# Counting kept context rows: adding six comparison tables on VectorE before TensorE sums them over the partitions

## The chip, the cores and the metric

The kernel runs on one NeuronCore of a Trainium2 chip. The metric is the device time of one execution in microseconds. The engines are TensorE (PE, its weight loads PEld), VectorE (DVE), ScalarE (ACT), GpSimd (POOL) and SyncE (SP); each has a queue of its own that it works through in order, and semaphores tie the queues together.

## The reference

A gated cross-attention block followed by a gated feed-forward network whose two layers have rounded activations and ternary weights. There are 16 batch elements with 224 tokens of width 512 and up to 750 context rows of width 384; a mask says for each batch element which context rows count. Cut to what matters:

```python
x = x + tanh(g_xattn[0]) * cross_attention(layernorm(x), ctx, mask, W_q, W_k, W_v, W_o, b_o)   # 8 heads of 64
x = x + tanh(g_ffn[0]) * ffn(layernorm(x), w1, b1, w2, b2)

# cross_attention
sim = einsum('bihd,bjhd->bhij', q, k) * scale
sim = where(mask[:, None, None, :], sim, max_neg)
out = einsum('bhij,bjhd->bihd', softmax(sim), v)

# ffn: twice a linear layer of this kind, with an exact gelu between them
xq = act_quant(rmsnorm(x))     # rounded to 255 levels per row
wq = weight_quant(w)           # rounded to -1, 0, 1 times the mean of |w|
einsum('bsd,fd->bsf', xq, wq) + b
```

Masked rows get a weight of zero, so only the kept rows of the context need be fetched and computed with.

## The kernel before, in words

**Ordering the batch.** `order_batches` (lines 30 to 159) counts the kept rows of each batch element, sorts the 16 elements by that count into slots, and gives each slot a capacity: 192 kept rows for the first eight slots, 128 for the last eight (`CAPS`, line 26). It also makes `sh.upto`: with the 750 rows laid out as 6 columns on 125 partitions, it holds for each row and slot how many rows are kept up to and including that row. If every slot fits its capacity, `compact_path` (from line 726) does the rest.

**select(s)** (line 809) turns these counts into the places of the kept rows. The place of the k-th kept row is the number of rows whose count is at most k. So for each of the six columns (`NJ`) a VectorE `tensor_scalar` compares the 192 or 128 possible places with the counts, one per partition (line 816, table `ind`, bf16, 125 partitions), and TensorE sums the tables over partitions and columns: the table is the stationary operand, a column of ones the moving one, and six matmuls with one moving column accumulate into one column of PSUM `pi` (line 822). A slot of 192 places takes two such columns (128 and 64 places), so 12 matmuls; one of 128 takes 6. Then `keys` (line 833) clips and shifts the sums to row numbers in memory, and `mask` (line 845) is the additive mask of the slot.

**gather(s)** (line 850) fetches the kept rows by indirect DMAs issued from GpSimd with `keys` as row numbers. The x rows (`fetch`, issued at line 793) and the results (line 1310) go through the same queue. `context_pieces` transposes the gathered rows (line 881) and computes the keys (892) and values (907, 918); `query_pieces` transposes x (987) and computes the queries (1008).

**Attention.** `scores` (line 1037) makes the score matmuls (1047), the masked minimum on VectorE (1061), the exponentials on ScalarE (1071), the reciprocal of the sum `rec` (1080) and the scaling of p on GpSimd (1081). `turn_probs` transposes p on TensorE (1101, 1108), `weighted` applies it to the values (1126, 1141).

**Feed-forward.** Finished tokens are taken in pairs of 128: `project` (1189, 1192), `normalise` (1226 to 1247), `up` (matmuls hp at 1259 into a wide PSUM tile, read by VectorE as `h` at 1267), `gelu` (1279 to 1298), `down` (1304, 1308).

**Weights.** w1 and w2 are loaded in eight pieces each; the first load waits until the first gathered context has landed (line 1347). Their absolute values are summed (1363, 1367, 1373), the scale `sw` comes from the sum (1375 to 1379), and each piece is rounded on VectorE (1396 to 1398) and turned on TensorE (1409, 1413).

**The order of the work.** select(0) and select(1) stand at the head of the compact path (lines 1464 and 1466), select(2) after the first sum of weights (line 1495), and stage s of the main loop (line 1505) holds select(s + 3), merged with the attention pieces of s, the queries and keys of s + 1, and the feed-forward or weight pieces. From this program order a planner makes the order of each engine's queue: an instruction whose operands and buffer it expects to be ready may pass earlier ones, and a buffer is handed on when its last reader is done. `ind` has one buffer, so the tables of a slot can only be built when the matmuls of the slot before have read theirs.

**The counters.** `evict` (line 757) sends each copy out of PSUM to VectorE or ScalarE, whichever has the smaller sum of charged work in `load`. Other code adds its own charges to `load["v"]` and `load["s"]` in program order; select adds 6 * 170 to `load["v"]`.

Of the kernel before, what the change touches and what calls it, by code (L numbers as in the profile page):

```python
# [9 lines left out]
BF16 = mybir.dt.bfloat16  # L10
AF = mybir.ActivationFunctionType
ALU = mybir.AluOpType
# [713 lines left out]
def compact_path(ctx, tc, sh, x, context, out, late_loads):  # L726

    nc = tc.nc
    P = 128
# [5 lines left out]
    NJ = 6  # L735
    TJ = J // NJ
# [12 lines left out]
    pa = ctx.enter_context(tc.tile_pool(name="pa", bufs=1))  # L749
# [3 lines left out]
    load = {"v": 0.0, "s": 0.0}  # L753
# [14 lines left out]
    def gen(shape, dtype, name):  # L768
        return ps_gen.tile(shape, dtype, tag="gen", name=name)
# [36 lines left out]
    def rows_of(s, t):  # L806
        return min(CAPS[s] - t * P, P)

    def select(s):

        st = live[s]
        cap = CAPS[s]
        nt = 2 if cap > P else 1
        ind = pa.tile([TJ, NJ, 192], BF16, tag="ind", name=f"ind_{s}", bufs=1)
        for n in range(NJ):
            nc.vector.tensor_scalar(ind[:, n, :cap], sh.place[:TJ, :cap], sh.upto[:, n, s : s + 1], None, ALU.is_ge)
        load["v"] += 6 * 170
        pi = gen([P, 2], F32, f"pi_{s}")
        for t in range(nt):
            rows = rows_of(s, t)  # L820
            for n in range(NJ):
                nc.tensor.matmul(
                    pi[:rows, t : t + 1],
                    lhsT=ind[:, n, t * P : t * P + rows],
                    rhs=sh.one[:, 0:1],
                    start=(n == 0),
                    stop=(n == NJ - 1),
                )

        keys = pa.tile([P, 2], I32, tag="keys", name=f"keys_{s}", bufs=3)  # L830
        for t in range(nt):
            rows = rows_of(s, t)
            nc.vector.tensor_scalar(
                keys[:rows, t : t + 1],
                pi[:rows, t : t + 1],
                float(J - 1),
                sh.first[:rows, s : s + 1],
                ALU.min,
                ALU.add,
            )  # L840
        st["keys"] = keys

        mb = pa.tile([TQ, 320], F32, tag="mask", name=f"mask_{s}", bufs=1)
        nm = 320 if nt > 1 else P
        nc.vector.tensor_scalar(
            mb[:, :nm], sh.place_f[:TQ, :nm], sh.slots[:TQ, 0, s : s + 1], -FMAX, ALU.is_ge, ALU.mult
        )
        st["mask"] = mb
# [613 lines left out]

    fetch(0)
    select(0)
    gather(0)
    select(1)
    norm_first(0)
    with tc.issue_after(norm_first(1)):
# [14 lines left out]
    with ExitStack() as behind:  # L1483
        for instruction in latest.values():
            behind.enter_context(tc.issue_after(instruction))
        scores(0, 0)
        scores(0, 1)
        for _, piece in queries[3:] + keys_values[3:]:
            piece()
        for c in range(NPC):  # L1490
            sum_weights(0, c)
        scale_weights(0)
        for _, piece in norm_pieces(1):
            piece()
        select(2)

        held = [sh.wo[0:1, 0, 0:1], sh.wo[0:1, 2, 0:1], sh.wo[P // 2 : P // 2 + 1, 2, 0:1]]
        for dst in held + [sh.bo[0:1, 0:1], sh.b1[0:1, 0:1], sh.b2[0:1, 0:1]]:
            nc.scalar.copy(dst, weight_sums[0][0:1, NPC - 1 : NPC])
# [85 lines left out]
```

## Time and profile before

| what | us |
|---|---|
| median of the three runs | 757.25 (756.26 to 759.62) |
| profiled execution, its own time | 755.32 |
| profiled execution, span from first to last instruction | 753.5 |
| busy: TensorE, VectorE, ScalarE, GpSimd | 680.1, 505.9, 407.6, 397.0 |
| granted TensorE clock, mean | 0.976 |

Line numbers with an L are those of the kernel before. A group's mean duration contains the time in which an instruction overlaps its neighbours, so the length of a block of like instructions is read from the timeline. A row of a timeline gives the start, the length, engine, line, operation, tiles and count, and in brackets the idle time of the engine ahead of it and what ended it.

### The profile page before, as it was taken

Reading aid. Unit: us, or ns where it says so; the run is one execution under the profiler, and the core shown is the slowest. Engines: PE = TensorE matmul, PEld = TensorE weight load, DVE = VectorE, ACT = ScalarE, POOL = GpSimd, SP = SyncE. Lnnn points to the kernel's source line nnn. Section 1 sums busy time; section 2 is a strip of 40 time slices with the busy share of each in tenths; the row PEclk is TensorE's granted clock in tenths of the full one; section 3 lists DMA queues with packets and bytes.
Section 4 is the critical chain, followed back from the end, with each engine's and each line's share of the span. In section 5 each row is a group of like instructions: output and inputs, shape, how many; then the busy total and the mean of one; then the engine's idle time right before and its main releaser. Section 6 shows DMA issues by size and latency. Waiting matters only on the chain.

```text
span 753.5 us, 11378 instructions
## 1 busy us (share of the span) xinstructions
PE 680.1 (90%) x3902; PEld 432.9 (57%) x3902; DVE 505.9 (67%) x1300; ACT 407.6 (54%) x960; POOL 397.0 (53%) x543
## 2 busy tenths in 40 slices
PE   4997799999999999997999999999999999988652
PEld 3875587666566566555655575666666666443221
DVE  5598765877484784665768676588594939586860
ACT  1556564384663855736657369266565656460530
POOL 6583567464564644647266564565654453536141
PEclk9998999999999999999999999999999999999887
DMA  6874031132223322222142323123122222213150
GB/s 193 314 267 156 11 90 45 15 73 56 69 47 70 82 56 57 67 57 81 28 99 67 71 67 68 32 77 80 58 57 70 56 70 57 71 28 77 35 113 31
DMA packets 87218, 58.77 MB, mean 78 GB/s; under 512 B 75488, under 2 KB 75632, under 8 KB 87024
## 3 DMA queue, kind: packets, MB, share of 16 engines
q1 hardware_dynamic: 79024, 32.00, 18.8%
q0 software_dynamic: 8128, 25.96, 11.1%
q8 instruction: 33, 0.54, 0.3%
q14 instruction: 33, 0.27, 0.1%
HBM read 32.26 MB, written 7.34 MB: 53 GB/s over the span
## 4 chain that ended last, share of the span: by engine, by line
PE 57%; DVE 12%; issue 10%; POOL 9%; DMA 5%; ACT 2%; POOLq 0%; ACTq 0%; DVEq 0%; SPq 0%
PE qp L1008 9%; PE op L1189 9%; PE fp L1304 8%; PE hp L1259 6%; PE kp L892 5%; PE sim L1047 4%; PE vp L907 4%; PE ptp L1101 3%; PE av L1126 3%; DVE a L1282 2%; POOL p L1081 2%; DVE h L1267 2%; DMA raw<-in_L_ffn_w_dram 2%; DMA hqT<-hq 2%; DVE hq L1285 1%
## 5 line engine op out<-in xcount | busy, mean ns | idle before, releaser
L1081 POOL TENSOR_TENSOR p<-p,rec 112x768 f32<-112x768 f32 (+1 forms) x64 | 84.2, 1318 | 74.8 <-DVE rec L1080 29.6
L1304 PE MATMUL fp<-w2T,hqT 128*128 128x512 fp8e4 x448 | 104.2, 387 | 13.8 <-DMA hqT<-hq 13.7
L1259 PE MATMUL hp<-w1T,xqT 128*128 128x512 fp8e4 x448 | 107.0, 383 | 8.8 <-DVE h L1267 6.2
L1071 ACT ACTIVATE p<-p,nm 112x192 f32<-112x192 f32 (+1 forms) x256 | 106.4, 419 | 11.5 <-DVE nm L1061 11.3
L1008 PE MATMUL qp<-xnT,wq_sb 128*128 128x224 f32 x512 | 104.9, 358 | 0.6 <-ACT xnT L766 0.6
L1189 PE MATMUL op<-wo_sb,xoT 128*128 128x512 f32 x224 | 103.7, 599 | 0.0
L1008 PEld LDWEIGHTS qp<-xnT,wq_sb 128*128 128x128 f32 x512 | 96.8, 193 | 6.4 <-issue 3.3
L1267 DVE SCALAR_TENSOR_TENSOR h<-hp,c,b_bc 128x1024 f32<-128x1024 f32 x56 | 71.6, 1280 | 39.9 <-PE hp L1259 37.4
L1061 DVE CUSTOM_DVE_ANT_0 p<-sim,mask 112x192 f32<-112x192 f32 (+1 forms) x256 | 67.7, 319 | 33.9 <-PE sim L1047 33.4
L1304 PEld LDWEIGHTS <-hqT 128*128 128x128 bf16 x448 | 43.3, 99 | 71.0 <-DMA hqT<-hq 16.9
L1282 DVE TENSOR_REDUCE a<-h 128x1 f32<-128x2048 f32 x28 | 63.9, 2282 | 22.4 <-ACT h L1279 22.3
L1259 PEld LDWEIGHTS <-xqT 128*128 128x128 bf16 x448 | 43.2, 98 | 57.7 <-issue 15.4
L1308 DVE SCALAR_TENSOR_TENSOR y<-fp,c,y 128x512 f32<-128x512 f32 x28 | 20.9, 746 | 76.3 <-PE fp L1304 73.0
L1310 POOL DMA_INDIRECT out_dram<-y,token x28 | 30.9, 1104 | 75.6 <-DVE y L1308 70.6
L1290 ACT ACTIVATE h<-h 128x2048 f32<-128x2048 f32 x28 | 53.4, 1907 | 22.1 <-DVE hq L1285 14.7
L1279 ACT ACTIVATE h<-h 128x2048 f32<-128x2048 f32 x28 | 53.5, 1909 | 19.6 <-DVE k L1200 10.6
L1189 PEld LDWEIGHTS op<-wo_sb,xoT 128*128 128x128 f32 x224 | 40.6, 190 | 38.9 <-issue 36.4
L892 PE MATMUL kp<-ctxT,wk_sb 128*128 128x192 f32 (+1 forms) x384 | 60.9, 306 | 0.0
L892 PEld LDWEIGHTS kp<-ctxT,wk_sb 128*128 128x128 f32 x384 | 55.2, 192 | 6.2 <-issue 4.3
L1247 POOL TENSOR_TENSOR y<-y,b_bc 128x512 f32<-128x512 f32 x28 | 36.6, 1311 | 37.9 <-DVE fx L1228 37.6
L766 ACT COPY pT<-ptp 128x448 f32<-128x448 f32 x63 | 32.7, 536 | 42.6 <-PE ptp L1101 41.3
L1101 PE MATMUL ptp<-ident,p 112*128 112x112 f32 x256 | 36.1, 268 | 17.6 <-POOL p L1081 17.5
(165 smaller groups left out, 1191.4 us busy)
## 6 DMA issues: line engine op xcount, KB each, us to landing
raw<-in_L_ffn_w_dram SPq DMA_DIRECT2D x16, 512.0 KB, 5.6
wq_sb<-in_L_xattn_W_q_dram SPq DMA_DIRECT2D x1, 1024.0 KB, 5.8
b_bc<-in_L_ffn_b_dram SPq DMA_DIRECT2D x1, 1024.0 KB, 7.8
wk_sb<-in_L_xattn_W_k_dram SPq DMA_DIRECT2D x1, 768.0 KB, 7.4
wv_sb<-in_L_xattn_W_v_dram SPq DMA_DIRECT2D x1, 768.0 KB, 8.8
wo_sb<-in_L_xattn_W_o_dram SPq DMA_DIRECT2D x1, 512.0 KB, 3.8
wo_sb<-in_L_xattn_W_o_dram SPq DMA_DIRECT2D x2, 256.0 KB, 5.6
x<-in_x_dram,token POOLq DMA_INDIRECT x28, 3.6
```

The lines of the kernel that those rows point to most:

```text
L892: nc.tensor.matmul(pk[:, p - p0, :], lhsT=sh.wk[:, c, p * P : (p + 1) * P], rhs=st["ctxT"][:, c, :cap], start=(c == 0), stop=(c == NC - 1),)
L1008: nc.tensor.matmul(pq[:, i, :], lhsT=sh.wq[:, d, (p + i) * P : (p + i + 1) * P], rhs=st["xnT"][:, d, :], start=(d == 0), stop=(d == ND - 1),)
L1061: nc.vector.tensor_tensor_reduce(out=probs[:, h, :cap], in0=sim[:, j, i, :cap], in1=st["mask"][:, j * begin : j * begin + cap], scale=-(DH ...
L1071: nc.scalar.activation(probs[:, h, :cap], probs[:, h, :cap], AF.Exp, bias=nmax, scale=-1.0, accum_out=total[:TQ, h : h + 1],)
L1081: nc.gpsimd.tensor_tensor(probs[:, :, :cap], probs[:, :, :cap], rec[:TQ].unsqueeze(2).to_broadcast([TQ, 4, cap]), ALU.mult,)
L1101: nc.tensor.transpose(pt[:, h, :], probs[:, h, c : c + P], ident[:TQ, :TQ])
L1189: nc.tensor.matmul(po, lhsT=xoT[:, d, at : at + P], rhs=sh.wo[:, d, :], start=(d == 0), stop=(d == ND - 1))
L1259: nc.tensor.matmul(ph[:, n, :], lhsT=f["xqT"][:, k * ND + d, :], rhs=w1T[:, d, at : at + NB], start=(d == 0), stop=(d == ND - 1),)
L1267: nc.vector.scalar_tensor_tensor(h[:, cols], ph.rearrange("t i n -> t (i n)"), f["c1", k], sh.b1[:, cols], ALU.mult, ALU.add)
L1279: nc.scalar.activation(f["h", k], f["h", k], AF.Gelu)
L1282: nc.vector.tensor_reduce(amax[:, k : k + 1], h, AX.X, ALU.max, apply_absolute_value=True)
L1304: nc.tensor.matmul(po, lhsT=f["hqT", k][:, n, :], rhs=w2T[:, n, :], start=(n == 0), stop=(n == NF - 1))
```

## The change

Instead of six tables side by side, one table is built. A `tensor_scalar` compares the places with the first column's counts; five `scalar_tensor_tensor` then each compare the places with the next column's counts and add the table so far, in place. The sums are small whole numbers (0 to 6), exact in bf16. TensorE then sums one table over the partitions, so a slot of 192 places takes two matmuls and one of 128 takes one. The table has two buffers in place of one (each a sixth of the former size), and select charges 6 * 260 to VectorE's counter in place of 6 * 170.

```diff
-        ind = pa.tile([TJ, NJ, 192], BF16, tag="ind", name=f"ind_{s}", bufs=1)
-        for n in range(NJ):
-            nc.vector.tensor_scalar(ind[:, n, :cap], sh.place[:TJ, :cap], sh.upto[:, n, s : s + 1], None, ALU.is_ge)
-        load["v"] += 6 * 170
+
+        ind = pa.tile([TJ, 192], BF16, tag="ind", name=f"ind_{s}", bufs=2)
+        nc.vector.tensor_scalar(ind[:, :cap], sh.place[:TJ, :cap], sh.upto[:, 0, s : s + 1], None, ALU.is_ge)
+        for n in range(1, NJ):
+            nc.vector.scalar_tensor_tensor(
+                ind[:, :cap], sh.place[:TJ, :cap], sh.upto[:, n, s : s + 1], ind[:, :cap], ALU.is_ge, ALU.add
+            )
+        load["v"] += 6 * 260
         pi = gen([P, 2], F32, f"pi_{s}")
         for t in range(nt):
             rows = rows_of(s, t)
-            for n in range(NJ):
-                nc.tensor.matmul(
-                    pi[:rows, t : t + 1],
-                    lhsT=ind[:, n, t * P : t * P + rows],
-                    rhs=sh.one[:, 0:1],
-                    start=(n == 0),
-                    stop=(n == NJ - 1),
-                )
+            nc.tensor.matmul(
+                pi[:rows, t : t + 1], lhsT=ind[:, t * P : t * P + rows], rhs=sh.one[:, 0:1], start=True, stop=True
+            )
```

## The prediction

> **What bounds the kernel now.** I read the page first (busy shares and the chain that ended last):
>
> ```profile
> PE 680.1 (90%) x3902; PEld 432.9 (57%) x3902; DVE 505.9 (67%) x1300; ACT 407.6 (54%) x960; POOL 397.0 (53%) x543
> ...
> PE 57%; DVE 12%; issue 10%; POOL 9%; DMA 5%; ACT 2%; POOLq 0%; ACTq 0%; DVEq 0%; SPq 0%
> ```
>
> TensorE is busy for 90% and carries 57% of the chain; VectorE carries 12%. An average says little, so next the busy time by stage (core, then length, then PE, weight load, VectorE, ScalarE, GpSimd):
>
> ```profile
> 37.20:46.40 9.20, 7.35 (x64) 5.01 (x64) 8.69 (x35) 2.52 (x10) 6.88 (x10) 1.00 0.83 268
> 46.40:157.00 110.60, 100.56 (x726) 76.30 (x727) 82.57 (x237) 64.27 (x176) 67.17 (x60) 0.95 0.28 82
> 157.00:540.00 383.00, 368.98 (x2103) 232.45 (x2102) 255.33 (x664) 227.84 (x536) 209.42 (x284) 1.00 0.28 65
> ```
>
> From 46 to 540 us TensorE is the bound (91% and 96%). From 37.2 to 46.4 us VectorE is (94%): the w1 weights have landed, and TensorE waits for the first rounded piece. After 540 us no select is left. Third, the tables and sums themselves, by tile:
>
> ```profile
> L822 PEld LDWEIGHTS <-ind x144: 95/98/157, 9.0 to 533.7; 125*128 125x128 bf16 x96, 125*64 125x64 bf16 x48
> L822 PE MATMUL pi<-one,ind x144: 163/170/210, 9.1 to 533.8; 125*128 125x1 bf16 x96, 125*64 125x1 bf16 x48
> L816 DVE TENSOR_SCALAR ind<-place,upto x96: 226/254/1780, 8.7 to 497.5; 125x192 bf16<-125x192 bf16 x48, 125x128 bf16<-125x128 bf16 x48
> ```
>
> 144 matmuls of 170 ns would be 24.5 us, which misleads: they overlap. TensorE's timeline gives what they occupy:
>
> ```profile
> 80.84 0.58 PE L822 MATMUL pi<-one,ind 125*128 125x1 bf16 x12
> 81.35 0.79 PE L881 MATMUL ctxp<-ident,ctx 128*128 128x128 f32 x3
> ```
>
> Twelve hold TensorE from 80.84 until the next matmul starts at 81.35, 0.51 us; in a later select six hold it from 244.31 to 244.47, 0.16 us. Last, VectorE's timeline in its own stage:
>
> ```profile
> 38.85 0.97 DVE L816 TENSOR_SCALAR ind<-place,upto 125x192 bf16<-125x192 bf16 x5
> 39.85 0.42 DVE L763 COPY v_rest<-vr 128x256 f32<-128x256 f32 x1
> 40.19 0.15 DVE L1377 TENSOR_SCALAR wmean<-wtotp 128x1 f32<-128x1 f32 x1
> ...
> 42.23 1.04 DVE L816 TENSOR_SCALAR ind<-place,upto 125x192 bf16<-125x192 bf16 x5
> 43.19 0.73 DVE L1396 TENSOR_SCALAR raw<-raw,sw 128x1024 f32<-128x1024 f32 x1
> 44.35 0.33 DVE L833 TENSOR_SCALAR keys<-pi,first 128x1 int32<-128x1 f32 x2 [0.43 <-PE pi L822]
> 44.61 0.68 DVE L1397 TENSOR_SCALAR w<-raw 128x1024 int16<-128x1024 f32 x1
> ```
>
> Two blocks of tables stand ahead of the weights here, and nothing hides them.
>
> [...]six of 192 columns take 1.17 us and six of 128 take 1.06, so 64 columns cost 18 ns each time. [...]The trace shows such blocks (3.65 and 4.00 us for six tables, at 433 and 494 us, while GpSimd ran tensor_tensors). [...]here (0.30-0.17)/5 = 26 ns in the blocks of six, (0.58-0.17)/11 = 37 ns in those of twelve.
>
> **The change, part by part.** Against the profiled execution: span 753.5 us, its own time 755.32; the median 757.25 is 1.9 above that, and I carry the difference over.
>
> *TensorE.* A select of the first eight goes from 12 matmuls to 2, of the last eight from 6 to 1. Saved: 0.51 less 2 x 0.04 = 0.43 us, and 0.16 less 0.04 = 0.12. Selects 0 to 3 lie where TensorE waits anyway (before 46 us): nothing, because the waits for the gathered context and the rounded weights cover it. Selects 4 to 6 (80.8, 116.8, 148.7 us): 3 x 0.43 x 0.91 = -1.2 us. Select 7 and the eight short ones: (0.43 + 8 x 0.12) x 0.96 = -1.3 us.
>
> *VectorE, price of the new instruction.* The trace has no such form between SBUF operands of this size. Scalar_tensor_tensor on 32 columns of SBUF takes 193 ns (L151), 512 columns 746 and 1024 columns 1280 (L1308, L1267, one input in PSUM): the slope is 1.043 ns a column. From the 193: 360 ns at 192 columns, 293 at 128. Bounds: down the slope from the 746, 412 and 345[...]. Each link waits for the one before: in the chain a dependent VectorE instruction follows 0.02 us after the one it needs (k at 223.63, its input done at 223.61). So a block is 0.27 + 5 x 0.38 = 2.17 us for 1.17, and 0.26 + 5 x 0.315 = 1.83 for 1.06: +1.00 eight times, +0.77 eight times, 14.2 us more VectorE work.
>
> *Where it lies.* Select 0: keys later by 1.00, less the 0.34 of matmuls no longer run after the last table (10.49 against 9.85, some 0.3 for the two that stay): 0.66 us. GpSimd, which issues the gather, is busy with the x fetches until 12.6 and starts it at 12.88, while keys are ready at 10.86: hidden in 2 us. Select 1 delays the first norm's statistics from 13.05 by 0.6; its next step stands behind the second tile's, which waits for its DMA until 15.03: hidden. Without these covers they cost 0.7 and 0.6. Two x fetches stretched to 1.26 and 1.52 us beside the tables, against 1.02 alone, may also shorten, by up to 0.7. I take 0 for the opening.
> Select 2: the block 38.60 to 39.82 grows by 0.96, and with it v_rest, wmean and sw. Select 3 by 0.87. L1396 comes 1.8 later, but the 0.43 that keys waits for pi is then covered: +1.4 us at L1397, the cast after it and TensorE's first turn of weights (46.34, which already waits 1.7).
> Selects 4 to 15: 4 x 1.00 + 8 x 0.77 = 10.2 us. Behind them in VectorE's queue stand rec (L1080), which frees GpSimd's product for the transposes of p, and h (L1267), which frees the wide PSUM tile for the hp matmuls. At 197 us the third hp starts 4 us after the h that it needs, and GpSimd's product stands behind a DMA wait, so most is hidden. I take VectorE's share of the chain, 12%: +1.2 us.
>
> *Planner and buffers.* Select charges 6 x 260 for 6 x 170. Walking the two counters in program order gives 21 evictions on VectorE before, as in the profile, and 15 after: 12 leave (about 5.3 us at their rows) and five come (3.0 us), all but one before 150 us. Net 2 us from VectorE to ScalarE (54% busy): 0. Two small tables instead of one large one add no DMA and no tile wait; they permit building a table a select earlier. The instruction order of each queue may be remade with that.
>
> Sum: 0 + 1.4 + 1.2 - 1.2 - 1.3 = +0.1 us, so 757.3.
>
> **The rivals.** *Faster (30%).* The second buffer takes select 3's block out of the 37 to 46 us stage (1.3 and the 0.43 wait), less select 2's 0.96: -0.8. The opening gains its 0.7, the chains of VectorE hide fully, TensorE gains all 2.7: -4.2 us, 753.0. If sw and L1396 are moved ahead of the blocks too, 3 us more, 750. For it: VectorE is busy for 10.2 of the 20.8 us from 16.4 to 37.2. Against: the order of today leaves ready work late as well (x fetched at 23 to 26 us has its statistics at 40.26).
> *Slower (24%).* [...]Place: between keys and h. Price: 2.6 to 2.9 us for a block of six at 433 and 494 us. Half of that, 1.4 us, reaching hp decides (3.8 us) from three such collisions beyond today's; four give +5.6, 763. Against: only two of sixteen blocks are hit so hard now, and part was hidden.
> *It doesn't do what it says.* If the matmuls taken out only let TensorE wait elsewhere, nothing stands against +1.4 and +1.2: 759.9, still within the forecast's range and counted there.
>
> **How the numbers follow.** Half a per cent, 3.8 us, is about what this measurement can tell from no change (the three runs span 3.4). Forecast 46%, with its own range 754.5 to 760.5 from the price bounds (5 x 0.05 us a block either way, and 0 to 25% of 10 us reaching the path). The cases of both signs push the range to 751 to 763, leaving a tenth on each side.
>
> **What would show it.** L822 with 24 matmuls; L816 with 16 and the new line with 80 of about 360 and 293 ns; VectorE's busy time up some 12 us (14.2 less 2.3), TensorE's down some 6 (2.7, and about 1 in each of the four selects that it runs while waiting); the first turn of weights near 47.7 us. Wrong if: [...]that turn comes earlier than 46.3; the new line's longest times exceed 1 us in more than three blocks; or the remade order moves a stage between 46 and 540 us by more than 3 us.

## The result and the profile after

The change makes the kernel slower: 778.28 us (776.21 to 781.14, six runs) against 756.75 (754.51 to 759.62, six runs), a ratio of 1.0284 with a 95% interval of 1.0259 to 1.0308. The profiled execution took 777.65 us, its span 775.9. Line numbers behind the change are one lower than before (L1081 is now L1080). The page of the kernel after, busy shares, granted clock and chain:

```profile
PE 687.3 (89%) x3782; PEld 435.6 (56%) x3782; DVE 516.3 (67%) x1294; ACT 408.6 (53%) x966; POOL 396.2 (51%) x543
...
PEclk9969799999999999899999999999999999998877
...
PE 48%; DVE 17%; issue 13%; POOL 11%; DMA 5%; ACT 4%; POOLq 0%; DVEq 0%; ACTq 0%; SPq 0%
```

TensorE runs 120 matmuls fewer and is still busy for 7.2 us longer, at a mean clock of 0.953 for 0.976. The span grew by 22.4 us, so 15.2 are new idle time of TensorE and 7.2 are slower matmuls, net of those that left. By stage (bounds moved with the work; columns as in the prediction):

```profile
37.20:50.50 13.30, 6.76 (x32) 3.35 (x30) 11.83 (x38) 6.70 (x25) 10.39 (x9) 0.74 0.57 162
50.50:164.00 113.50, 104.42 (x714) 79.29 (x715) 85.82 (x231) 65.23 (x181) 66.20 (x63) 0.93 0.26 83
164.00:558.00 394.00, 372.88 (x2050) 234.53 (x2049) 255.87 (x659) 228.34 (x536) 208.37 (x282) 0.98 0.26 63
```

The losses are spread: the opening (4.1 us and then 2.9), the long middle (394 us for 383), and 4.4 us after it. The table itself, by tile (min, median and max in ns):

```profile
L818 DVE SCALAR_TENSOR_TENSOR ind<-place,upto,ind x80: 314/405/2098, 9.1 to 489.3; 125x192 bf16<-125x192 bf16 x40, 125x128 bf16<-125x128 bf16 x40
...
L825 PE MATMUL pi<-one,ind x24: 163/178/214, 12.3 to 551.5; 125*128 125x1 bf16 x16, 125*64 125x1 bf16 x8
L816 DVE TENSOR_SCALAR ind<-place,upto x16: 238/254/1239, 8.7 to 485.9; 125x192 bf16<-125x192 bf16 x8, 125x128 bf16<-125x128 bf16 x8
```

The counts are as written in the change. So where did the 22 us come from? Two places show most of it. First, the stage from 306 to 359 us (292 to 341 before). GpSimd's timeline before, and then after:

```profile
297.30 1.27 POOL L1182 TENSOR_TENSOR y<-y,bo_bc 128x512 f32<-128x512 f32 x1 [1.14 <-DMA y<-in_x_dram,token]
298.53 1.47 POOL L1081 TENSOR_TENSOR p<-p,rec 112x768 f32<-112x768 f32 x1
300.14 1.04 POOL L793 DMA_INDIRECT x<-in_x_dram,token  x1
301.48 1.01 POOL L793 DMA_INDIRECT x<-in_x_dram,token  x1 [0.30 <-issue]
```

```profile
312.16 1.27 POOL L1181 TENSOR_TENSOR y<-y,bo_bc 128x512 f32<-128x512 f32 x1 [2.43 <-DMA y<-in_x_dram,token]
313.58 1.00 POOL L793 DMA_INDIRECT x<-in_x_dram,token  x1
314.89 1.01 POOL L793 DMA_INDIRECT x<-in_x_dram,token  x1 [0.30 <-issue]
315.91 1.48 POOL L1080 TENSOR_TENSOR p<-p,rec 112x768 f32<-112x768 f32 x1
```

The queue's order is another one: the two fetches of x now stand ahead of the scaling of p. And the wait for y (rows of x, fetched once more to be added to the result) ahead of both is 2.43 us in place of 1.14. TensorE stands at the transposes of p (tile `ptp`), before and after:

```profile
300.05 0.60 PE L1101 MATMUL ptp<-ident,p 112*128 112x112 f32 x4 [0.16 <-POOL p L1081]
300.68 1.89 PE L1259 MATMUL hp<-w1T,xqT 128*128 128x512 fp8e4 x8
```

```profile
317.45 1.01 PE L1100 MATMUL ptp<-ident,p 112*128 112x112 f32 x4 [4.11 <-POOL p L1080]
318.63 3.62 PE L1258 MATMUL hp<-w1T,xqT 128*128 128x512 fp8e4 x8
```

A wait of 4.11 us for 0.16, and then the same eight matmuls take 3.62 us for 1.89. The record of the granted clock in the trace is at one half from 316.6 to 323.5 us, from within the wait until past the eight matmuls. The stretches at half clock inside this span last 13.7, 10.2, 3.4, 3.4, 6.8, 3.4, 6.8, 6.8 and 10.2 us, all multiples of 3.4, and a last one is cut off by the end. So this wait is paid for twice. The same holds for the whole stretch: from slot 7 to slot 10 (the starts of their pi matmuls, 195.40 to 340.73 before, 203.17 to 359.31 after) TensorE's idle time grew from 5.1 to 11.0 us and its busy time from 140.2 to 145.1.

Second, the opening. VectorE's timeline after, and the two waits of TensorE there:

```profile
42.37 0.13 DVE L1372 TENSOR_REDUCE wtot<-wsums 128x1 f32<-128x8 f32 x1
...
44.24 1.40 DVE L1395 TENSOR_SCALAR raw<-raw,sw 128x1024 f32<-128x1024 f32 x2
```

```profile
42.64 0.35 PE L1374 MATMUL wtotp<-wtot,ones 128*128 128x1 f32 x2 [2.53 <-DVE wtot L1372]
...
50.82 1.12 PE L986 MATMUL xnp<-ident,x 128*128 128x128 f32 x4 [3.89 <-POOL x L960]
```

The tables of selects 2 and 3 are no longer here; their first links now stand at 16 to 20 us. But the masked minima of slot 0's scores were put ahead of the last sums of weights, so TensorE waits for the sum, then 3.9 us for x, and the clock is at one half from 43.6 to 57.2 us. TensorE's first turn of weights, before and then after, comes 7.7 us later:

```profile
46.34 0.62 PE L1409 MATMUL wp<-ident,w 128*128 128x128 bf16 x8 [1.66 <-DVE w L1398]
```

```profile
54.05 1.04 PE L1408 MATMUL wp<-ident,w 128*128 128x128 bf16 x8
```

The two waits are not a pure loss, since a longer one of the kernel before has gone:

```profile
62.90 1.01 PE L1101 MATMUL ptp<-ident,p 112*128 112x112 f32 x4 [5.08 <-POOL p L1081]
```

From 37.2 us to the same work at 81.0 us before and 84.9 after, TensorE's idle time is 6.9 and 7.7 us and its busy time 36.9 and 40.0, at a clock of 0.92 and 0.86. So most of what these 44 us lost is slower matmuls, and the clock here also differs between two profiles of one and the same program: from 37.2 us to slot 7 it is 0.97 before, 0.93 after, and 0.93 in e5 below, which runs the instructions of before.

### The profile page after: what moved, and what is told of

It reads as the page before. It is cut to its first block, busy times and chain, and to the rows that moved or that the text cites. A ratio compares the mean times of both kernels' runs of the same rounds, so it can differ in the third digit from the quotient of the medians.

```text
span 775.9 us, 11140 instructions
## 1 busy us (share of the span) xinstructions
PE 687.3 (89%) x3782; PEld 435.6 (56%) x3782; DVE 516.3 (67%) x1294; ACT 408.6 (53%) x966; POOL 396.2 (51%) x543
## 4 chain that ended last, share of the span: by engine, by line
PE 48%; DVE 17%; issue 13%; POOL 11%; DMA 5%; ACT 4%; POOLq 0%; DVEq 0%; ACTq 0%; SPq 0%
PE op L1188 8%; PE qp L1007 8%; PE fp L1303 7%; PE hp L1258 6%; PE kp L891 4%; PE sim L1046 4%; PE vp L906 3%; PE ptp L1100 2%; POOL p L1080 2%; DVE h L1266 2%; DVE a L1281 2%; PE av L1125 2%; ACT p L1070 2%; DVE ind L818 2%; DMA hqT<-hq 2%
## 5 line engine op out<-in xcount | busy, mean ns | idle before, releaser
L1080 POOL TENSOR_TENSOR p<-p,rec 112x768 f32<-112x768 f32 (+1 forms) x64 | 84.2, 1317 | 80.0 <-DVE rec L1079 50.2
L1303 PE MATMUL fp<-w2T,hqT 128*128 128x512 fp8e4 x448 | 107.5, 396 | 14.8 <-DMA hqT<-hq 14.8
L1258 PE MATMUL hp<-w1T,xqT 128*128 128x512 fp8e4 x448 | 109.6, 390 | 7.8 <-DVE h L1266 5.4
L1188 PEld LDWEIGHTS op<-wo_sb,xoT 128*128 128x128 f32 x224 | 40.7, 190 | 38.8 <-issue 36.3
L1100 PE MATMUL ptp<-ident,p 112*128 112x112 f32 x256 | 36.6, 271 | 21.5 <-POOL p L1080 20.0
```

What stands on the lines that cost most here:

```text
L1080: nc.gpsimd.tensor_tensor(probs[:, :, :cap], probs[:, :, :cap], rec[:TQ].unsqueeze(2).to_broadcast([TQ, 4, cap]), ALU.mult,)
L1188: nc.tensor.matmul(po, lhsT=xoT[:, d, at : at + P], rhs=sh.wo[:, d, :], start=(d == 0), stop=(d == ND - 1))
L1258: nc.tensor.matmul(ph[:, n, :], lhsT=f["xqT"][:, k * ND + d, :], rhs=w1T[:, d, at : at + NB], start=(d == 0), stop=(d == ND - 1),)
L1303: nc.tensor.matmul(po, lhsT=f["hqT", k][:, n, :], rhs=w2T[:, n, :], start=(n == 0), stop=(n == NF - 1))
```

## The experiments

Three causes were open: the queue orders, the additions on VectorE, and the new charge to the counter. To separate them the kernels marked "held" fix a queue's order: edges that add no semaphore tie each instruction of a queue to its successor in a given order.

```diff
     for _, piece in weave(up_pieces(i), downs[:2]) + downs[2:]:
         piece()
+    in_order(tc, queue_order())
```

All times are compared with the kernel before on the same chip.

**First set: orders, arithmetic or charge.** e1 is the change (with the old charge, so that the evictions stay as they were), all four queues held in the order of before; the one matmul stands where the first of its six stood.

> The changed kernel's arithmetic (one table, five dependent additions, one matmul for six, two buffers), but with the charge of 6 * 170 (so the PSUM evictions go to the same engines as before) and with the instructions of TensorE, VectorE, ScalarE and GpSimd held in the queue order of the kernel before (the one matmul stands where the first of the six stood). Theory O, the loss comes from the remade queue order: 751 to 758 us, no slower than before, perhaps 1 to 3 us faster by the matmuls taken out. Theory C, the loss comes from the longer chains on VectorE themselves, which delay rec and h and collide with GpSimd: 768 us or more.

Measured: 767.01 us, ratio 1.0160 [1.0095, 1.0225], between the two expectations.

e2 is the opposite: the old six tables and six matmuls, with two buffers and the new charge, in the queue orders of the kernel after.

> The arithmetic of the kernel before (six tables, six matmuls), with the charge of 6 * 260, two buffers, and the four queues held in the order of the changed kernel. Theory O: 770 to 782 us, nearly the whole loss without any of the new instructions. Theory C: 755 to 760 us.

Measured: 774.14 us, 1.0258 [1.0199, 1.0317]. With the old arithmetic, the new orders alone give nearly the whole loss.

e3 is the kernel after with one number changed.

```diff
-        load["v"] += 6 * 260
+        load["v"] += 6 * 170
```

> The changed kernel with select's charge back at 6 * 170, nothing else. All 320 PSUM evictions then go where they went before; GpSimd's queue keeps the three remade stages (between 203 and 359 us). Theory K, the charge and the 17 evictions that it moves are the cause: 755 to 761 us. Theory O with GpSimd's three stages as its main part: the 10.8 us lost there stay, what was lost before 203 us may go, 764 to 775 us. Theory C: 775 to 780 us.

Measured: 776.48 us, 1.0284 [1.0222, 1.0346]: the charge is not it. The time lies where theory C put it, but e2 has just spoken against C.

e4 is the kernel after with GpSimd's queue alone held in the order of before.

> The changed kernel as it is, with GpSimd's queue alone held in the order of the kernel before (the scaling of p ahead of the x fetches and the second addition of the bias). Theory O with GpSimd's queue as the main part: the three stages between 203 and 359 us get back most of their 10.8 us and TensorE's waits of 3.5 and 4.1 us for p there go, 764 to 770 us. Theory C: VectorE delays p whatever the order on GpSimd, 775 to 780 us.

Measured: 770.47 us, 1.0202 [1.0145, 1.0258]. GpSimd's order is a part: TensorE's longest wait for p between slots 7 and 10 is 1.5 us again.

But e1 and e2 don't add up: the orders gave 2.6%, the arithmetic without them 1.6%, both together 2.8%. Either the two losses overlap, or something else was in e1.

**Second set: the two halves in the old order.** e5 is the control, the kernel before held in its own order.

> The kernel before, with the order of its four queues (TensorE, VectorE, ScalarE, GpSimd) held as it already is; nothing else. Every theory expects no change, 755 us give or take 2, with a span of 753 to 756 us. If it comes out at 760 us or more, holding an order costs time by itself, and the runs of the first set that held one have to be read again. Its profile is also a second look at one and the same program: the stretch after the last pi took 219.9 us in the first[...].

Measured: 756.67 us, 0.9992 [0.9964, 1.0020]: holding costs nothing. Its profiled execution, instruction for instruction the program before, had a span of 760.2 us for 753.5, and 59.9 us of it at half clock for 36.3. So one profile against another means little below some 7 us at the end; the ratios decide.

e6 is VectorE's half: the additions, and six matmuls that each write the whole sum (edited from the kernel after).

```diff
-            nc.tensor.matmul(
-                pi[:rows, t : t + 1], lhsT=ind[:, t * P : t * P + rows], rhs=sh.one[:, 0:1], start=True, stop=True
-            )
+            for n in range(NJ):
+                nc.tensor.matmul(
+                    pi[:rows, t : t + 1], lhsT=ind[:, t * P : t * P + rows], rhs=sh.one[:, 0:1], start=True, stop=True
+                )
```

> VectorE's half of the change alone, in the queue orders of before: the sum is made by the five dependent additions, and TensorE still runs six matmuls per column, each of which writes the whole sum again, so that the output stays the reference's. Theory V (in the old order it is the additions that cost, by holding keys and the weights behind them, and by TensorE's waits): 764 to 771 us, as with both halves (767). Theory M (VectorE's half is hidden, and the 120 matmuls that left had kept TensorE busy, so that without them its clock falls): 754 to 758 us.

Measured: 761.93 us, 1.0059 [1.0033, 1.0086], between the two expectations.

e7 is TensorE's half: six tables as before, one matmul (edited from the kernel before).

```diff
-            for n in range(NJ):
-                nc.tensor.matmul(
-                    pi[:rows, t : t + 1],
-                    lhsT=ind[:, n, t * P : t * P + rows],
-                    rhs=sh.one[:, 0:1],
-                    start=(n == 0),
-                    stop=(n == NJ - 1),
-                )
+            nc.tensor.matmul(
+                pi[:rows, t : t + 1],
+                lhsT=ind[:, 0, t * P : t * P + rows],
+                rhs=sh.one[:, 0:1],
+                start=True,
+                stop=True,
+            )
```

> TensorE's half alone, in the queue orders of before: VectorE still makes six tables, TensorE sums only the first over the partitions and the other five are left out, so other tokens are chosen and the output is another one; as many rows are gathered as before. Theory V: 752 to 756 us, since 120 matmuls of 0.03 us or less leave and nothing is added. Theory M: 762 to 768 us.

Measured: 765.49 us, 1.0126 [1.0097, 1.0155]. Taking matmuls away, with nothing added and every queue in its old order, costs 9.5 us. Theory V had excluded that; theory M gave the size, but its cause had still to be shown.

e8 is the change with the old charge, GpSimd's and VectorE's queues held in the order of before.

> The kernel after, with its charge at the 170 of before (776.5 us in the first set), GpSimd's and VectorE's queues held in the order of before, TensorE's and ScalarE's as they come. Held GpSimd alone gave 770.5 us, all four held 767.0. If the two queues carry the whole effect of the order, 766 to 769 us, TensorE's wait for ptp in the stages from 254 to 359 us back under 0.5 us and TensorE's wait for wtotp back under 0.5 us. If TensorE's or ScalarE's own order counts, 770 to 776 us.

Measured: 761.69 us, 1.0087 [1.0063, 1.0111], less than expected: TensorE's and ScalarE's own orders are no worse for being remade. The two waits that the expectation wanted under 0.5 us are not: 2.0 us for `wtotp` (the sum of the weights), and up to 1.6 us each for ptp between slots 7 and 10. In the kernel before they are 1.1 us and up to 1.5 us, so that sign was set too low.

**What e7 showed.** In e7, GpSimd's wait for y at 201 us is 2.77 us (1.00 before). The DMA view of e7 from 200 to 204 us has, beside the rows of y, one packet of another queue:

```profile
q0 software_dynamic: 160, 0.52, 44.0%
q8 instruction: 1, 0.02, 1.8%
```

The trace calls it a queue of instructions. Its packets have 16,384 bytes each, 33 of them in the kernel before and 32 in every kernel with one matmul. Between two of them lie some 250 recorded matmuls and weight loads (the median). In the kernel after it is 198 to 292 of these between each two of the first 30 packets, but 15 to 72 instructions of VectorE and 13 to 53 of ScalarE: the packets go with TensorE's stream, and I read them as the fetches of its instructions. With 10 or 20 such instructions fewer in each select, the fetches slide along the work, and in all kernels with one matmul (after, e1, e3, e4, e7, e8) they came beside fetches of y between 200 and 365 us; in those with six matmuls (before, e2, e5, e6) beside none of these. Beside one, y kept GpSimd waiting for 1.7 to 2.8 us where it was the last to arrive; without one, for 0.99 to 1.25. The exceptions are the third and fourth fetch in e7 (1.17 and 1.53 us): the packet had ended at 301.34 us, just ahead of y's first at 301.36, and in the fourth it was half done (349.42 to 350.52) when y's came (350.07).

**Third set: moving the fetches.** The edit adds work: 44 matmuls of one column, where TensorE waits for the first context rows; the transposes overwrite what they write.

```diff
             pt = gen([P, c1 - c0, cap], F32, f"ctxp_{s}_{c0}")
+            if s == 0 and c0 == 0:
+                for _ in range(44):
+                    nc.tensor.matmul(
+                        pt[:, 0, 0:1], lhsT=sh.place[:TJ, :P], rhs=sh.one[:, 0:1], start=True, stop=True
+                    )
```

> The kernel of e7 (TensorE's half alone, 765.5 us) with 44 further matmuls of one column each put in front of the first ctxp transposes, where TensorE waits 3.6 us for the first context rows; they are overwritten by the transposes. Theory F: TensorE's instructions are themselves fetched by DMA, 16,384 bytes each 19 to 31 us (32 such packets in e7, 33 in the kernel before), and with 120 matmuls fewer these fetches fall into the fetch of y in the four stages from 200 to 350 us, so that y lands 0.4 to 1.7 us later (GpSimd waits 2.77, 1.79, 1.17, 1.53 us for it; 1.00 to 1.24 before). The 88 instructions more move the fetches about 9 us ahead of y: GpSimd's wait back to 1.0 to 1.25 us in all four, and the time 754 to 758 us although work was added. Theory D (other rows are gathered, or fewer matmuls leave TensorE's clock lower): no change, 764 to 768 us.

Measured for e9: 757.11 us, 1.0008 [0.9988, 1.0028], for 1.0126 without the 44. GpSimd's timeline, e7 and then e9:

```profile
203.75 1.27 POOL L1227 TENSOR_TENSOR y<-y,bo_bc 128x512 f32<-128x512 f32 x1 [2.77 <-DMA y<-in_x_dram,token]
```

```profile
200.30 1.28 POOL L1232 TENSOR_TENSOR y<-y,bo_bc 128x512 f32<-128x512 f32 x1 [1.21 <-DMA y<-in_x_dram,token]
```

The other three waits are 1.09, 1.12 and 1.02 us, as foretold.

> The kernel before in its own order, with the same 44 matmuls in the same idle time. Theory F: its instruction fetches, now at 208, 258, 305 and 352 us, move to about 199, 249, 295 and 342 us, where y is fetched (issued by 199.2, 248.1, 296.2, 344.5 us); two or three of the four fetches of y land later, and the time grows by 2 to 6 us, to 757 to 761. Theory D: the matmuls stand in an idle time, 755 us give or take 2.

Measured for e10: 758.61 us, 1.0003 [0.9981, 1.0026]. Two of the four fetches of y landed later, at the places named:

```profile
252.30 1.28 POOL L1233 TENSOR_TENSOR y<-y,bo_bc 128x512 f32<-128x512 f32 x1 [2.06 <-DMA y<-in_x_dram,token]
```

(2.20 us at 303 us, 1.07 and 1.09 in the other two.) That part held; the measured time did not follow. So two late fetches of y are not by themselves worth more than 2 us; the expectation of 757 to 761 named the right microseconds only because before, too, took 758.49 on that chip. The run also shows that the 44 matmuls by themselves do nothing to the time. The profile does show what they are worth: set against e5, which has the same instructions but for the 44, e10 falls 1.0 us further behind at each of the two late fetches. A late y thus costs about its lateness, and two of them are as much as this measurement can miss.

> The kernel after with all its own queue orders, and the same 44 matmuls. Theory F: GpSimd's wait for y in the four stages back from 1.8 to 2.4 us to 1.0 to 1.3, and the time falls from 778 to 768 to 774 us. Theory D: 776 to 780 us.

Measured for e11: 774.44 us, 1.0227 [1.0159, 1.0295]: y's four waits are 1.21, 1.21, 1.12 and 1.03 us, and most of the loss stays.

> The kernel of e1 (both halves of the change in the queue orders of before, 767.0 us) with the same 44 matmuls. Theory F: as VectorE's half alone (762), less the matmuls that left: 758 to 763 us. Theory D: 765 to 769 us.

Measured for e12: 758.94 us, 1.0009 [0.9990, 1.0028], for 1.0160 without the 44.

So in the old order, with the fetches out of the way, the change itself costs nothing that can be measured. Where the 9.5 us of e7 go is told only in part by the profiles of e7 and e9 (7.2 us apart): 2.3 between slots 7 and 10, where y is late (1.6 and 0.8 us at the first two fetches, which were 1.6 and 0.7 later); 1.9 up to slot 7, with one more stretch at half clock (64.0 to 70.8 us); 2.8 after slot 15. There, the 24th of e7's 28 groups of `fp` (the matmuls of the second feed-forward layer) waits for `hqT` (its input, transposed by DMA), with a packet of instructions at 686.2 us beside its transpose:

```profile
688.32 5.31 PE L1349 MATMUL fp<-w2T,hqT 128*128 128x512 fp8e4 x16 [3.48 <-DMA hqT<-hq]
```

In e9 that group doesn't wait for hqT; the one before it waits 2.33 us, for 1.42 in e7. The other kernels tell the same: in all six with one matmul and without the 44 (after, e1, e3, e4, e7, e8) the 24th group waits 3.44 to 3.48 us, with a packet that began 2.11 us before the end of the wait. In the eleven others the packet lies elsewhere, and the group waits 1.85 us at most. What follows the last pi takes 3.0 to 6.0 us longer than before in the six, and 0.2 less to 2.5 more in the eleven. So the packet delays this transpose, too.

One run doesn't fit. e6 has none of these meetings and still costs 0.6%, clear of the noise. Its profile has the whole loss by slot 7 (7.1 us behind before there, and 7.1 at the end). A part is a chain that meets GpSimd's work (tensor_tensors from 126.01 to 128.82 us), behind which TensorE waits for y, as it does in the kernel after (1.3 us at 129.64) but not before:

```profile
125.08 4.41 DVE L864 SCALAR_TENSOR_TENSOR ind<-place,upto,ind 125x192 bf16<-125x192 bf16 x5
...
130.49 0.29 PE L1147 MATMUL ptp<-ident,p 112*128 112x112 f32 x1 [1.46 <-DVE y L1238]
```

The rest stays open; e6 was not run with the 44.

**Fourth set: which queue's order, without the fetches.** e13, e14 and e15 are the change with the old charge and the 44 matmuls; held in the order of before are GpSimd's and VectorE's queues, GpSimd's alone, VectorE's alone.

> The kernel of e8 (the change with the charge of 170; GpSimd's and VectorE's queues in the order of before, TensorE's and ScalarE's as they come; 1.0087 of before) with the 44 matmuls in the idle time ahead of the first ctxp. If these two queues carry the whole effect of the orders: 0.995 to 1.003 of before (752 to 760 us), with GpSimd's wait for y at 1.0 to 1.3 us in the stages from 200 to 350 us. If TensorE's or ScalarE's order counts too: 1.005 or more.

> The change with the charge of 170, GpSimd's queue alone in the order of before, with the 44 matmuls. Theory G (the new orders cost because GpSimd fetches x ahead of scaling p): 0.998 to 1.006 of before, as VectorE's order then costs little. Theory H (they cost because VectorE takes h ahead of rec, and GpSimd only waits for rec): 1.012 to 1.022.

> The same with VectorE's queue alone in the order of before and GpSimd's as it comes, with the 44 matmuls. Theory G: 1.012 to 1.022 of before. Theory H: 0.998 to 1.006.

Measured: e13 757.38 us, 1.0003 [0.9984, 1.0023]; e14 763.85, 1.0063 [1.0020, 1.0106]; e15 765.89, 1.0115 [1.0072, 1.0158]. Theory H is out: both intervals lie clear of its ranges. G's ranges are missed by 0.0003 and 0.0005, well inside the noise; but e14's interval lies above 1, so VectorE's order costs something as well. How far each profile is behind the kernel before at the pi matmuls of slots 7 and 10 and at the end (us), and TensorE's wait for ptp between slots 7 and 10 (4.1 before):

| kernel | slot 7 | slot 10 | end | wait for ptp |
|---|---|---|---|---|
| after | +7.8 | +18.6 | +22.4 | 10.8 |
| e11, both queues new | +10.3 | +21.5 | +20.8 | 9.5 |
| e14, VectorE's new | +10.8 | +9.7 | +8.6 | 4.8 |
| e15, GpSimd's new | +2.7 | +7.8 | +9.6 | 7.4 |
| e13, both old | +0.8 | 0.0 | +1.1 | 4.6 |

By these profiles VectorE's new order is paid for before slot 7, in the opening. (In all six profiles with it, after, e2, e3, e4, e11 and e14, slot 7 is 5.6 to 10.8 us behind; with the old one it is 3.6 at most, but for e6 with its 7.1.) GpSimd's is paid for between slots 7 and 10, where x goes ahead of p: 5.1 us in e15, and 11.2 in e11, where VectorE's is new as well. There the two make each other worse. TensorE's waits from slot 7 to slot 10 in e11, and then in e13:

```profile
PE ptp L1152 <- POOL p L1132: 9.5, 4, 2.8
```

```profile
PE ptp L1151 <- POOL p L1131: 4.6, 4, 1.5
```

e13, the version that might have beaten both kernels, ties with the kernel before. None of the fifteen versions is clearly faster.

## Why the prediction was wrong

**The step that failed is "Planner and buffers: 0".** It had the net of the evictions right (VectorE 1300 to 1294 instructions, six fewer; its 12 and five would make seven), saw that "the instruction order of each queue may be remade", named it among the things that would make the forecast wrong, and gave it no price. It is the largest term: 2.3% or 17 us (e11), and nothing in its absence (e13). One of its signs of being wrong was a stage between 46 and 540 us moved by more than 3 us: the long middle moved by 11. What set the new order off is in the programs as the planner orders them. Two buffers in the kernel before change no queue, and its charge alone doesn't move p. Each half of the change alone, with one buffer, the old charge and no order held, puts p behind the fetches of x in these stages: the additions with six matmuls do, and so do the six tables with one matmul. So it is not the longer VectorE work alone; which of the planner's expected times tips the order stays open.

**No step priced the instruction fetches.** The rest of the loss, some 0.6% in the new orders (2.84 less 2.27, which their intervals alone don't separate) and 0.8 to 1.5% in the old ones (e8 against e13, e7 against e9, e1 against e12, all apart), came with 120 matmuls and their weight loads leaving TensorE's stream, and left when 44 matmuls were added. The forecast had them as a gain. Late fetches of y and of hqT are seen where the packets fall; they tell some 5 of the 7.2 us between e7 and e9.

**The sum, term by term.** *The price of the new instruction* was too low: a link takes 0.45 us at 192 columns and 0.38 at 128 (five in 2.23 to 2.28 and in 1.90 us in e12, in blocks without a long link), forecast 0.38 and 0.315, and with the same 0.02 us between links 0.43 and 0.365 at its upper bound. A part of it is the wait for the link before: where two chains alternate in the kernel after, eight links of 192 columns take 2.71 us, one each 0.33. By shape the rows of the tables add up to 45.8 us for 25.6, so 20.2 us more and not 14.2. *The opening, 0*: almost. The second buffer let the chains of selects 0 and 1 interleave, so that keys came at 12.65 for 10.53 us and the first ctxp at 16.80 for 16.23. *The stage from 37 to 46 us, +1.4*: the first piece of weights was scaled at 44.24 for 43.19, but behind the scores; the two blocks had left. The stage grew by 4.1 us, and TensorE turned that piece at 54.05 us, for 47.7 forecast, behind its waits of 2.5 and 3.9 us. *Chains later on, +1.2*: in the old order not measurable in the whole change (e12, e13), although some blocks of e12 ran as long as those beside GpSimd's tensor_tensors in e6 (four links in 1.81 us at 156, but five in 4.21 at 123 and in 5.17 at 440; in e6 4.41 at 125 and 5.26 at 440); VectorE's half alone, e6, costs 4.5 us, by its profile mostly ahead of 110 us. *TensorE, -2.5*: not there either. (The forecast's 26 and 37 ns are from one start to the next within a block of such matmuls.) e9 has the whole saving and stands at 0.9988 at best, 0.9 us. That the matmuls only held TensorE where it would have waited, as the forecast's last rival has it, fits, but is not shown. The sum of +0.1 us is what e12 and e13 measure. That is luck: neither +1.4, +1.2 nor -2.5 is seen there one by one.

**The rivals.** The slower one had the sign, and a small part of the mechanism: of the collisions between the chains and GpSimd, the one at 125 us makes TensorE wait 1.3 us in the kernel after and 1.5 in e6, but the one at 440 us in e6 (five links in 5.26 us) leaves the lag behind before as it was. The faster one foresaw the second buffer taking the blocks out of the opening; that came true, and the stage grew.

## What to carry to other kernels

Where an order is planned from expected durations, a change of a few instructions is two changes: hold the old order with the new instructions (e12 here), and the new order with the old ones (e2), before saying what the instructions cost. Where instructions leave an engine's stream, look at where its instruction fetches fall afterwards: here 120 matmuls and their loads fewer on TensorE put packets beside y and hqT, and 44 more with theirs took them away again (e7, e9). If a time moves without a cause in any queue, look at the packets of the instruction queue beside the small transfers that are waited for. A wait of TensorE can cost more than its length: here 4.11 us, and then 1.73 us more for the eight matmuls behind it, at a clock of one half.

## What the runs showed of the hardware that I had not expected

- TensorE's instruction fetches (16,384 bytes each, in the kernel before one each 18 to 28 us from 146 to 649 us) delayed a fetch of 128 rows beside them: GpSimd waited 2.77 us with one (e7) and 1.21 without (e9). They delayed a transpose by DMA as well: TensorE waited 3.44 to 3.48 us for hqT in six kernels with a packet beside it, 1.85 at most in eleven without. Putting 88 instructions more ahead of them took 1.2% off e7 and 1.5% off e1. In e10 it made two fetches late, at 1.0 us each by the profiles, and no difference in the medians.
- The same program, run 63 times in one set, took 752.0 to 763.9 us; in its two profiles the clock was at one half for 36.3 and 59.9 us of the span.
- A single link of the chained addition, with 128 columns and its operands in SBUF, took from 314 to 2098 ns in the kernel after, and from 393 to 1548 ns with 192. The eleven links above 1 us ran beside a tensor_tensor of GpSimd for 0.86 to 1.47 us each; the others took 432 ns at most, with 0.33 us beside one at most.
